# Softmax results of a three-part attention kernel sent to device memory two at a time, and the tiles that hold them

## The chip, the cores and the metric

The kernel runs on one core of a Trainium2 chip. A core has four compute engines, TensorE (PE, matrix products), VectorE (DVE), ScalarE (ACT) and GpSimd (POOL), and SyncE (SP), whose queue issues nearly all transfers here. Sixteen DMA engines carry those out. The time is the device time of one execution in microseconds (us), given as the median of several runs. A profile is taken of one more execution.

## The reference

Sixteen sequences of 128 tokens with 512 features, all in 32-bit floats, go through a decoder layer and then a gated cross attention.

```python
# decoder layer
ln_out = layernorm(hidden_states, ln1_s, ln1_b)
q, k, v = jnp.split(ln_out @ w_qkv + b_qkv, 3, axis=-1)
x = hidden_states + merge_heads(attention(split_heads(q), split_heads(k), split_heads(v), ltor_mask)) @ w_ao + b_ao
ln_out = layernorm(x, ln2_s, ln2_b)
q = ln_out @ w_q + b_q
k, v = jnp.split(encoder_states @ w_kv + b_kv, 2, axis=-1)
x = x + merge_heads(attention(split_heads(q), split_heads(k), split_heads(v), cross_mask)) @ w_co + b_co
x = x + gelu(layernorm(x, ln3_s, ln3_b) @ w1 + b1) @ w2 + b2
# gated cross attention
a = _layer_norm(audio_kv, ln_gamma, ln_beta)
Q, K, V = x @ Wq.T, a @ Wk.T, a @ Wv.T
attn = softmax(where(mask, Q K^T * scale, -inf))
return x + tanh(gate) * ((attn V) @ Wo.T)
```

There are 16 heads of 32 features, and the hidden layer of the MLP has 2,048. `attention` scales the scores, adds a mask, takes a softmax over the keys and multiplies by the values.

## The kernel before

**Stages.** The sequences form four groups of four batches. The decoder's self-attention (sections A0 to A3), its cross attention (B0 to B3), the MLP (C0 to C3) and the gated attention (D0 to D3) follow each other; a section is one group in one attention. A is on the chip from the start to about 300 us, B to about 540, the MLP to about 945, D to the end. Every engine runs its instructions in the order in which the program lists them (class `InOrder`, line 36), so a wait holds up all that stands behind it on the same engine. Many large products are made of seven products of quarters instead of eight, with sums of quarters made beforehand on GpSimd or VectorE (`left_blocks`, `right_blocks`, `token_sums`, lines 346 to 363 and 1004 to 1011).

**Units and steps.** `attend` (line 662) walks through the softmax in steps. A batch has four units, each 128 queries by four heads by 128 keys (128 x 512 numbers, 256 KB); a step begins one unit. For the unit begun in step k:

- at the first step of a batch, TensorE makes the scores of all four units into four banks (`scores`, 523); the next batch's scores need those banks again;
- VectorE scales (and, in D, masks) the scores into a tile of the tag `s` (`scale_unit`, 540). The steps in which a batch's units are scaled stand in `SCALED` (658): unit 0 in the first, 1 and 2 in the second, 3 in the third. In A and B, GpSimd adds the mask in step k;
- in step k+1 ScalarE takes the exponents (`exp_unit`, 560), in k+2 VectorE inverts the sums and GpSimd divides (`norm_unit`, 569), in k+3 VectorE transposes 32 x 32 blocks in place and SyncE writes the tile to device memory (`turn_unit`, 575);
- in step k+5 of an odd unit SyncE reads the pair back with the blocks rearranged (`receive_pair`, 598), which completes the transpose, and TensorE multiplies by the values ten steps after the batch's first (`mix`, 609), into the product `av`.

The last batch of all is transposed by TensorE instead (`turn_by_array`, 585). The block sizes of a write follow from the tile, `[128, 4, 4, 32]`: each of 128 partitions sends four pieces of 128 numbers, 512 bytes.

**Tiles of the tag `s`.** Seven tiles of 2 KB a partition go round in the order of their requests. A request waits until the last reader of the tile's former content is done, for a softmax unit the landing of its write. Besides the units, the MLP's quarters of token sums (`sums_of`, 1067), its quarters of results (`projected_out`, 1172), four transposed hidden states of the last gated group (1412) and the last batch's own tiles take from the same seven.

**Around the MLP's start.** The MLP is a generator whose first pieces are run inside the last cross-attention section (`beside_last_cross`, 1601). In the last step of that section's sixteen, GpSimd makes the first of the token sums (`sx`), in between that step's and the next step's softmax work; the products `h` take them as operands. Its operands are the first group's normalized tokens (`T_C`) and its weights (`w`, and `t` for their sums).

Of the kernel before, what the change touches and what calls it, by code (L numbers as in the profile page):

```python
# [10 lines left out]
F32 = mybir.dt.float32  # L11
# [5 lines left out]
P = 128  # L17
NB = 16
S = 128
Q = 32  # L20
NQ = S // Q
# [3 lines left out]
KC = H // P  # L25
# [28 lines left out]
def decoder_then_gated_cross_attention(ctx: ExitStack, tc: tile.TileContext, a: dict, out: bass.AP):  # L54
    nc = InOrder(tc)
# [3 lines left out]
    work = ctx.enter_context(tc.tile_pool(name="work", bufs=1))  # L59
    dram = ctx.enter_context(tc.tile_pool(name="dram", bufs=1, space=bass.MemoryType.DRAM))  # L60
# [47 lines left out]
    x = [cpool.tile([P, GB, H], F32, tag=f"x{g}", name=f"x{g}") for g in range(NG)]  # L108
# [228 lines left out]
    HF = TG // 2  # L337
# [2 lines left out]

        return [[t[:, 2 * i : 2 * i + 2, j * HF : (j + 1) * HF] for j in range(2)] for i in range(2)]

    def quarter(pool, tag, name, bufs):
        return pool.tile([P, 2, HF], F32, tag=tag, name=name, bufs=bufs)

    def left_blocks(wt, t):


        (a11, a21), (a12, a22) = halves(wt)
        s3, s2, s4, s1 = (*t, a21)[:4]  # L350
        return [a11, a12, s4, a22, s1, s2, s3], [
            (s3, a11, a21, ALU.subtract), (s1, a21, a22, ALU.add), (s2, s1, a11, ALU.subtract),
            (s4, a12, s2, ALU.subtract),
        ]
# [161 lines left out]
    class Batch:  # L516
        def __init__(self, sec, b):
            self.sec, self.b, self.name = sec, b, f"{sec.name}_{b}"

            self.by_array = sec.at_end and b == GB - 1  # L520
            self.sc, self.s, self.mn, self.sum, self.away, self.pT = {}, {}, {}, {}, {}, {}

    def scores(bt):
        sec, t = bt.sec, slice(bt.b * S, (bt.b + 1) * S)
# [12 lines left out]
    def by_head(t):  # L537
        return t.rearrange("p n c j -> p c n j")

    def scale_unit(bt, j):  # L540
        s = work.tile([P, NQ, KC, Q], F32, tag="s", name=f"s_{bt.name}_{j}", bufs=7)
        if bt.by_array:
            s = s.rearrange("p n c j -> p (n c j)").rearrange("p (c n j) -> p n c j", c=KC, n=NQ)
        bt.s[j] = s
        sc = bt.sc.pop(j).rearrange("p (c n k) -> p c n k", c=KC, n=NQ)
        if bt.sec.adds_only:
            bt.mn[j] = least_tile(bt, j)
            bt.sec.mask_and_least(by_head(s), sc, bt.b, bt.mn[j])
        else:
            bt.sec.scale_mask(by_head(s), sc, bt.b)  # L550
# [24 lines left out]
    def turn_unit(bt, j):  # L575
        s = bt.s.pop(j)
        nc.vector.transpose(s, s)

        if j % 2 == 0:
            bt.away[j // 2] = dram.tile([NQ, P, 2, KC * Q], F32, tag="away", name=f"away_{bt.name}_{j}", bufs=4)  # L580
        nc.sync.dma_start(
            out=bt.away[j // 2][:, :, j % 2].rearrange("m p x -> p m x"), in_=s.rearrange("p m c q -> p m (c q)")
        )

    def turn_by_array(bt, j):

        s = by_head(bt.s.pop(j)).rearrange("p c n k -> p c (n k)")
        tp = ps("sc", f"tp_{bt.name}_{j}")
        for c in range(KC):
            nc.tensor.transpose(tp[:, c * S : (c + 1) * S], s[:, c], ident)  # L590
        pT = work.tile([P, KC, NQ, Q], F32, tag="s", name=f"pT_{bt.name}_{j}", bufs=7)
        bt.pT[j] = pT.rearrange("p c n q -> p n c q")
        if j % 2:
            afterwards("act", lambda: nc.scalar.copy(pT.rearrange("p c n q -> p (c n q)"), tp))
        else:
            afterwards("dve", lambda: nc.vector.tensor_copy(pT.rearrange("p c n q -> p (c n q)"), tp))
# [12 lines left out]
    def mix(bt):  # L609
        sec, b = bt.sec, bt.b  # L610
        av = ps("mm", f"av_{bt.name}")
        for c in range(KC):
            for j in range(GB):
                h = c * GB + j
                nc.tensor.matmul(
                    av[j * HD : (j + 1) * HD, c * S : (c + 1) * S], sec.v[:, b, h * HD : (h + 1) * HD],
                    bt.pT[j][:, :, c, :], start=True, stop=True,
                )
        mT = work.tile([P, KC, S], F32, tag="s", name=f"mT_{bt.name}", bufs=7) if bt.by_array else sec.mixed_tile(b)

        def mixed_out():
            if sec.v_bias is None:
                nc.scalar.copy(mT, av.rearrange("p (c q) -> p c q", q=S))
            else:
                for c in range(KC):
                    nc.scalar.activation(
                        mT[:, c], av[:, c * S : (c + 1) * S], AF.Identity, bias=col(sec.v_bias[0], sec.v_bias[1] + c)
                    )

        afterwards("act", mixed_out)  # L630
        bt.mT = mT
# [23 lines left out]
                out.setdefault(step, []).append(job)  # L655
        return out

    SCALED = ((0,), (1, 2), (3,), ())
    NS = GB * GB
    PRODUCTS = [m + GB * b for b in range(GB) for m in (1, 2, 3)]  # L660

    def attend(sections, ready, others, after=None):
# [14 lines left out]
        def step(k, bt=None, jobs=(), ahead=None):  # L677
# [45 lines left out]
            if bt is not None:  # L723
                for j in SCALED[m]:
                    scale_unit(bt, j)
# [332 lines left out]
    def mlp(ml, last_steps):  # L1058

        def turned_tile(g):  # L1060
# [3 lines left out]
                return [t[:, 0:2], t[:, 2:4]]  # L1064
            return [work.tile([P, 2, TG], F32, tag="mask", name=f"T_C{g}_{n}", bufs=2) for n in range(2)]

        def sums_of(g, t):
            s3, s2, s4 = (quarter(work, "s", f"sx{n}_{g}", 7) for n in range(3))
            quarters = [[t[i][:, :, j * HF : (j + 1) * HF] for j in range(2)] for i in range(2)]
            return token_sums(quarters, s3, s2, s4)  # L1070

# [100 lines left out]
        def projected_out(g, p, mm, acc):  # L1172
            mm = mm.rearrange("p (b n) -> p b n", n=HF)
            (x11, x12), (x21, x22) = halves(x[g])
            add, gadd = nc.vector.tensor_tensor, nc.gpsimd.tensor_tensor
            if p == 0:
                acc["m1"] = quarter(work, "s", f"m1_{g}", 7)
                add(acc["m1"], mm, half_row(ml.b2), ALU.add)
                gadd(x11, x11, acc["m1"], ALU.add)
            elif p == 1:  # L1180
                add(x11, mm, x11, ALU.add)
            elif p == 3:
                add(x21, x21, mm, ALU.subtract)
            elif p == 5:
                acc["u2"] = quarter(work, "s", f"u2_{g}", 7)
                add(acc["u2"], mm, acc["m1"], ALU.add)
                gadd(x12, x12, acc["u2"], ALU.add)
            elif p == 6:
                acc["u3"] = quarter(work, "s", f"u3_{g}", 7)
                add(acc["u3"], mm, acc["u2"], ALU.add)  # L1190
                gadd(x21, x21, acc["u3"], ALU.add)
                gadd(x22, x22, acc["u3"], ALU.add)
            elif p == 4:
                m5 = quarter(work, "s", f"m5_{g}", 7)
                add(m5, mm, half_row(ml.db2), ALU.add)
                gadd(x12, x12, m5, ALU.add)
                gadd(x22, x22, m5, ALU.add)
            elif p == 2:
                add(x12, mm, x12, ALU.add)
# [16 lines left out]
        before, acc = None, {}  # L1216
        for n in range(len(steps) + 1):
# [6 lines left out]
            if n < len(steps):  # L1224
                g, i = steps[n]
# [27 lines left out]
            for r in range(7):  # L1253
                if n < len(steps):
                    p = H_ORDER[r]
                    hidden_product(n, p, sides[p], right1[n][p], h)
                if before is not None:
                    p = O_ORDER[r]
# [15 lines left out]
            if n < len(steps):  # L1274
                t = work.tile([P, 3, 2, HF], F32, tag="kT", name=f"sh_{n}", bufs=2)
# [113 lines left out]
    class GatedAttention(Section):  # L1389
# [11 lines left out]

        def hidden_states(self, b, tag="pT"):

            t = work.tile([P, NQ, KC, Q], F32, tag=tag, name=f"x_{self.name}_{b}", bufs=3 if tag == "pT" else 7)
            nc.vector.transpose(by_chunk(t), squares(x[self.g][:, b, :]))
            send(self.x_away, t, b)

        def prepare(self, p):

            g = self.g  # L1410
            if g == 2 and p in (6, 8, 10, 12):
                gates[3].hidden_states(p // 2 - 3, "s")
            if g == 2 and p in (7, 9, 11, 13):
                gates[3].add_void((p - 7) // 2)

            if p in (1, 7):
                self.back, self.part = receiver("xa"[p == 7] + str(g), self.a_away if p == 7 else self.x_away)
            if p in (1, 3, 7, 9):
                for m in range(2):
                    self.part(m + 2 * (p in (3, 9)))  # L1420
            elif p == 4:
                self.xT = act_tile(self.name, "actT" if g == 3 else "enc")
            elif p in (5, 6):
                self.take_hidden(range(2 * (p - 5), 2 * (p - 4)))
# [171 lines left out]
    gates = [GatedAttention(g) for g in range(NG)]  # L1596
# [111 lines left out]
```

## Time and profile before

| | |
|---|---|
| median of three runs | 1166.22 us (1162.94 to 1170.1) |
| the profiled execution | 1168.78 us, span of its instructions 1167.0 |
| granted TensorE clock, mean | 0.994 |
| writes of softmax units | 188 of 256 KB, landing after 3.0 (A), 5.2 (B), 3.7 (D) us in the median |
| reads of pairs | 4 x 94 of 128 KB, 3.0 (A), 3.6 (B), 2.8 (D) us |
| moved by DMA | 259.80 MB, 223 GB/s |

The median landing times are those of the issues whose landing the page could match. The page names instructions by what they write and read: `s_B<-s_B,mask` is a unit of a cross-attention section to which the mask is added, `away_B<-s_B` its write, `pT_B<-away_B` its read. Nearly all instructions bear line 50, the helper that records them, so they are told apart by these names. "PE busy" includes the time in which a matmul runs at a lowered clock; the row PEclk of the slices, or of a window, tells the share of the full clock that was granted. SyncE's instructions only issue; the landing of a transfer is what others wait for.

### The profile page before, as it was taken

What the parts mean: (1) busy time and instruction counts of PE and PEld (TensorE: products, weight loads), DVE (VectorE), ACT (ScalarE), POOL (GpSimd) and SP (SyncE); (2) the same over time, 40 slices, a digit from 0 to 9 for tenths busy, and PEclk for the clock granted to TensorE, in tenths of its full rate; (3) what the DMA queues carried; (4) which work ended last, traced back from release to release, by engine and by line L of the source; (5) the groups of instructions that cost most, each with busy time, mean ns of one, the idle gap of its engine ahead of it and who ended that gap; (6) DMA issues with size and microseconds to landing.
All of it is one profiled execution on the core that took longest, in us unless ns stands there. A gap on an engine that the chain in (4) does not pass through costs nothing. (4 is left out here: it accounts for less than half of the span.)

```text
span 1167.0 us, 22047 instructions
## 1 busy us (share of the span) xinstructions
PE 1134.5 (97%) x7210; PEld 868.3 (74%) x7210; DVE 739.2 (63%) x1894; ACT 605.6 (52%) x2132; POOL 701.5 (60%) x636
## 2 busy tenths in 40 slices
PE   7999999999999999998999999999999999999988
PEld 5877777657575757545788888888888777878866
DVE  7678878797878877876663633543432247767753
ACT  2467667666666766674221333232222247867653
POOL 7698878688868776684333424433341367545973
PEclk9999999999999999999999999999999999999989
DMA  6598979999889879898796696696457728988964
GB/s 227 148 221 220 240 188 222 248 235 267 199 229 208 239 202 255 243 290 252 264 287 235 188 273 197 193 301 224 154 184 249 211 48 229 249 215 251 264 191 163
DMA packets 325266, 259.80 MB, mean 223 GB/s; under 512 B 83544, under 2 KB 280608, under 8 KB 320288
## 3 DMA queue, kind: packets, MB, share of 16 engines
q1 hardware_dynamic: 325112, 258.38, 78.0%
q8 instruction: 58, 0.95, 0.3%
q14 instruction: 56, 0.46, 0.1%
q10 hardware_dynamic: 40, 0.01, 0.0%
HBM read 163.94 MB, written 94.37 MB: 221 GB/s over the span
## 5 line engine op out<-in xcount | busy, mean ns | idle before, releaser
L50 ACT ACTIVATE s_A<-s_A,mn_A 128x128 f32<-128x128 f32 x256 | 99.5, 393 | 51.5 <-issue 37.3
L50 DVE TENSOR_TENSOR h<-h,h 128x512 f32<-128x512 f32 x80 | 54.9, 686 | 112.6 <-PE h L50 112.6
L50 ACT ACTIVATE s_B<-s_B,mn_B 128x128 f32<-128x128 f32 x256 | 99.5, 393 | 46.6 <-issue 32.5
L50 ACT ACTIVATE h<-h 128x512 f32<-128x512 f32 x64 | 40.3, 630 | 160.6 <-DVE h L50 160.6
L50 POOL TENSOR_TENSOR s_D<-s_D,sum_D 128x512 f32<-128x512 f32 x64 | 66.5, 1040 | 67.8 <-DVE sum_D L50 66.3
L50 ACT ACTIVATE s_D<-s_D,mn_D 128x128 f32<-128x128 f32 x256 | 99.2, 392 | 0.4 <-issue 0.4
L50 POOL TENSOR_TENSOR s_B<-s_B,sum_B 128x512 f32<-128x512 f32 x64 | 66.8, 1045 | 48.7 <-DVE sum_B L50 44.3
L50 POOL TENSOR_TENSOR s_A<-s_A,sum_A 128x512 f32<-128x512 f32 x64 | 66.6, 1041 | 36.0 <-DVE sum_A L50 35.3
L50 POOL TENSOR_TENSOR s_A<-s_A,ma 128x512 f32<-128x512 f32 x64 | 81.9, 1280 | 5.4 <-DVE s_A L50 3.7
L50 POOL TENSOR_TENSOR s_B<-s_B,mask 128x512 f32<-128x512 f32 x64 | 81.3, 1270 | 2.1 <-DMA away_B<-s_B 0.4
L50 POOL TENSOR_TENSOR rstd_aD<-rstd_aD,mhalf 128x1 f32<-128x1 f32 x12 | 6.6, 548 | 114.6 <-DVE rstd_aD L50 101.1
L50 POOL TENSOR_TENSOR sh<-h 128x512 f32<-128x512 f32 x32 | 40.7, 1272 | 50.9 <-ACT h L50 43.0
L50 PE MATMUL mo_B<-w_co,mT_B 128*128 128x512 f32 x128 | 60.5, 616 | 2.1 <-ACT mT_B L50 2.1
L50 PE MATMUL h<-T_C,t 128*128 128x256 f32 x256 | 60.7, 380 | 1.4 <-DVE h L50 1.4
L50 PE MATMUL h<-T_C,w 128*128 128x256 f32 x256 | 61.0, 381 | 0.8 <-DVE h L50 0.8
L50 PE MATMUL h<-sx,t 128*128 128x256 f32 x256 | 60.6, 380 | 0.0
L50 PE MATMUL o<-w,h 128*128 128x256 f32 x256 | 60.5, 379 | 0.0
L50 PE MATMUL o<-t,h 128*128 128x256 f32 x256 | 60.5, 379 | 0.0
L50 PE MATMUL o<-t,sh 128*128 128x256 f32 x256 | 60.5, 379 | 0.0
L50 PE MATMUL mo_A<-w_ao,mT_A 128*128 128x512 f32 x128 | 59.1, 604 | 0.0
L50 DVE CUSTOM_DVE_ANT_0 s_D<-sc_D,gmask 128x128 f32<-128x128 f32 x256 | 57.2, 283 | 0.9 <-DMA turned_x<-x_D 0.9
L50 PE MATMUL mm_q_B<-T_B,w_cq 128*128 128x512 f32 x128 | 57.3, 595 | 0.0
(324 smaller groups left out, 2986.1 us busy)
## 6 DMA issues: line engine op xcount, KB each, us to landing
t<-kept SPq DMA_DIRECT2D x24, 1024.0 KB, 6.9
away_A<-s_A SPq DMA_DIRECT2D x64, 256.0 KB, 3.0
pT_A<-away_A SPq DMA_DIRECT2D x128, 128.0 KB, 3.0
away_B<-s_B SPq DMA_DIRECT2D x64, 256.0 KB, 5.2
pT_B<-away_B SPq DMA_DIRECT2D x128, 128.0 KB, 3.6
away_D<-s_D SPq DMA_DIRECT2D x60, 256.0 KB, 3.7
pT_D<-away_D SPq DMA_DIRECT2D x120, 128.0 KB, 2.8
w<-in_L_xattn_w_dram SPq DMA_DIRECT2D x24, 512.0 KB, 5.6
```

The lines of the kernel that those rows point to most:

```text
L50: return lambda *args, **kw: self.tc.keep_in_program_order(call(*args, **kw))
```

## The change

A tile of the tag `s` now holds two units, and there are three such tiles (12 KB a partition). The seventh 2 KB have a tag of their own, `xh`, with one tile, taken in turn by one of the MLP's quarters, by the four transposed hidden states, and by the last batch's mixed values. The two units of a pair lie beside each other within each of four blocks, so that one write of 512 KB, issued after the odd unit's transpose, takes both in pieces of 1,024 bytes; the even unit's write, a step earlier, is gone. `SCALED` moves unit 2 of a batch from its second to its third step. In the MLP the quarters no longer go round: groups 0 and 2 have three fixed places and groups 1 and 3 three others, and the result quarters m1, u2, u3 and m5 of a group take the places of its token sums.

```diff
     def scale_unit(bt, j):
-        s = work.tile([P, NQ, KC, Q], F32, tag="s", name=f"s_{bt.name}_{j}", bufs=7)
-        if bt.by_array:
-            s = s.rearrange("p n c j -> p (n c j)").rearrange("p (c n j) -> p n c j", c=KC, n=NQ)
+        if j % 2 == 0:
+            shape = [P, 2, KC, NQ, Q] if bt.by_array else [P, NQ, 2, KC, Q]
+            bt.pair = work.tile(shape, F32, tag="s", name=f"s_{bt.name}_{j}", bufs=3)
+        s = bt.pair[:, j % 2].rearrange("p c n j -> p n c j") if bt.by_array else bt.pair[:, :, j % 2]
+        bt.pair_of[j] = bt.pair
         bt.s[j] = s
...
         nc.vector.transpose(s, s)
-        if j % 2 == 0:
-            bt.away[j // 2] = dram.tile([NQ, P, 2, KC * Q], F32, tag="away", name=f"away_{bt.name}_{j}", bufs=4)
-        nc.sync.dma_start(
-            out=bt.away[j // 2][:, :, j % 2].rearrange("m p x -> p m x"), in_=s.rearrange("p m c q -> p m (c q)")
-        )
+        pair = bt.pair_of.pop(j)
+        if j % 2:
+            away = dram.tile([NQ, P, 2, KC * Q], F32, tag="away", name=f"away_{bt.name}_{j}", bufs=4)
+            nc.sync.dma_start(
+                out=away.rearrange("m p u x -> p m (u x)"), in_=pair.rearrange("p m u c q -> p m (u c q)")
+            )
+            bt.away[j // 2] = away
...
-    SCALED = ((0,), (1, 2), (3,), ())
+    SCALED = ((0,), (1,), (2, 3), ())
...
+        places = []
+
+        def place(g, n):
+            return places[3 * (g % 2) + n]
+
         def sums_of(g, t):
-            s3, s2, s4 = (quarter(work, "s", f"sx{n}_{g}", 7) for n in range(3))
+            if g < 2:
+                for n in range(1 + g):
+                    t2 = work.tile([P, 2, 2, HF], F32, tag="s", name=f"sx_{g}_{n}", bufs=3)
+                    places.extend((t2[:, 0], t2[:, 1]))
+                if g == 0:
+                    places.append(work.tile([P, 2, HF], F32, tag="xh", name="sx_0", bufs=1))
+            s3, s2, s4 = place(g, 0), place(g, 1), place(g, 2)
...
-                acc["m1"] = quarter(work, "s", f"m1_{g}", 7)
+                acc["m1"] = place(g, 0)
...
-                acc["u2"] = quarter(work, "s", f"u2_{g}", 7)
+                acc["u2"] = place(g, 1)
...
-                acc["u3"] = quarter(work, "s", f"u3_{g}", 7)
+                acc["u3"] = place(g, 2)
...
-                m5 = quarter(work, "s", f"m5_{g}", 7)
+                m5 = place(g, 0)
...
-            t = work.tile([P, NQ, KC, Q], F32, tag=tag, name=f"x_{self.name}_{b}", bufs=3 if tag == "pT" else 7)
+            t = work.tile([P, NQ, KC, Q], F32, tag=tag, name=f"x_{self.name}_{b}", bufs=3 if tag == "pT" else 1)
...
-                gates[3].hidden_states(p // 2 - 3, "s")
+                gates[3].hidden_states(p // 2 - 3, "xh")
```

The last batch's transposed pairs (`pT` in `turn_by_array`) take two-unit tiles of the tag `s` in the same manner, and its `mT` takes `xh`.

More of the change, by code (lines that the diff above doesn't have):

```diff
@@ L341, in halves @@
         return [[t[:, 2 * i : 2 * i + 2, j * HF : (j + 1) * HF] for j in range(2)] for i in range(2)]
-    def quarter(pool, tag, name, bufs):
-        return pool.tile([P, 2, HF], F32, tag=tag, name=name, bufs=bufs)
     def left_blocks(wt, t):
@@ L520, in __init__ @@
             self.by_array = sec.at_end and b == GB - 1
-            self.sc, self.s, self.mn, self.sum, self.away, self.pT = {}, {}, {}, {}, {}, {}
+            self.sc, self.s, self.mn, self.sum, self.away, self.pT, self.pair_of = {}, {}, {}, {}, {}, {}, {}
     def scores(bt):
@@ L590, in turn_by_array @@
             nc.tensor.transpose(tp[:, c * S : (c + 1) * S], s[:, c], ident)
-        pT = work.tile([P, KC, NQ, Q], F32, tag="s", name=f"pT_{bt.name}_{j}", bufs=7)
+        if j % 2 == 0:
+            bt.pair = work.tile([P, 2, KC, NQ, Q], F32, tag="s", name=f"pT_{bt.name}_{j}", bufs=3)
+        pT = bt.pair[:, j % 2]
         bt.pT[j] = pT.rearrange("p c n q -> p n c q")
@@ L618, in mix @@
                 )
-        mT = work.tile([P, KC, S], F32, tag="s", name=f"mT_{bt.name}", bufs=7) if bt.by_array else sec.mixed_tile(b)
+        mT = work.tile([P, KC, S], F32, tag="xh", name=f"mT_{bt.name}", bufs=1) if bt.by_array else sec.mixed_tile(b)
         def mixed_out():
```

## The prediction

> **What bounds the kernel now.** I read the busy sums first, then the slices, then TensorE's waits, and at last the order in time around the places where TensorE stops.
>
> ```profile
> PE 1134.5 (97%) x7210; PEld 868.3 (74%) x7210; DVE 739.2 (63%) x1894; ACT 605.6 (52%) x2132; POOL 701.5 (60%) x636
> DMA  6598979999889879898796696696457728988964
> ```
>
> TensorE works 1134.5 of 1167.0 us; 32.5 us are its gaps. Some 7 us of them are the start (4.4 us for the first load, the rest for the first transposes) and are not touched, so some 25 us could be won by any change, plus what a slow clock costs after a gap. The second line shows where the 16 DMA engines are nearly full: windows of 20 us give a DMA share of 0.97 to 1.03 at 220 to 280 and 480 to 520 us, and of 0.97 to 0.98 at 1000 to 1040. From 580 to 940 us (the MLP) TensorE is busy 360.00 of 360 us: nothing can be won there.
>
> TensorE's own waits (engine, what it waited for, us, times, longest):
>
> ```profile
> PE sc_D L50 <- DVE mn_D L50: 4.3, 3, 3.2
> PE av_D L50 <- DMA pT_D<-away_D: 3.3, 2, 2.7
> PE av_B L50 <- DMA pT_B<-away_B: 2.4, 2, 1.6
> PE mo_B L50 <- ACT mT_B L50: 2.1, 1, 2.1
> ```
>
> Only 5.7 us are waits for the softmax results' way through device memory, the thing that the change makes cheaper. The first line is VectorE's scaling of scores, which the change delays for one unit in four.
>
> **1. The transfers, part by part.** Before, 188 writes of 256 KB in pieces of 512 bytes; after, 94 of 512 KB in pieces of 1,024. By the trace's packets a piece of 512 bytes takes 27 ns (median), one of 1,024 bytes 46 ns. 188 x 512 pieces x 27 ns / 16 engines = 162 us; 94 x 512 x 46 / 16 = 138 us: 24 us less of 16 engines' time, 0.26 us a pair. Steps last 3.8 us in the decoder and 3.1 us in the gated part (the scalings' spacing), a pair two of them, so the load falls by 3 to 4%. SyncE issues 94 instructions less, 0.38 us each, but most stood in time in which SyncE waited for a landing anyway.
>
> [...]
>
> What a pair's landing does: the odd unit's write now carries both, so where the queue was empty it lands 46 x 32 - 27 x 32 = 0.6 us later; where the queue was full the even unit's 0.86 us no longer stand ahead and it lands 0.26 us sooner. The reads are unchanged. The reads of a pair land 4 to 8 us ahead of their matmuls in most batches of the decoder, so 0.6 us is covered there. In the gated part five batches have under 0.7 us to spare or none; bounds -0.3 to +0.6 each, -1.5 to +3 us; I take +0.5.
>
> **2. Three tiles of two instead of seven of one.** Before, a unit's tile was free again three or four steps after its write; now the pair scaled from step 2i needs the write issued at step 2i-2 to have landed. I matched VectorE's scalings and transposes and SyncE's writes by their order. In the 90 pairs with a predecessor, the landing that a pair would need comes after its scaling 13 times, by 9.2 us in all (decoder 3.7, gated 5.4); with 0.6 us more for each landing the sum is 18.4. But they come in groups (82 to 96, 265 to 281, 490 to 525, 987 to 1030 us) where SyncE itself lags 2 to 5 us behind the transposes, and within a group one wait serves for all: the largest are 0.8, 1.5, 0.6 and 2.0, 5 to 7 us of VectorE's waiting. Behind a waiting scaling stand the next step's evictions and transposes. VectorE is busy 63% and comes to its evictions before TensorE does, so a wait under 1.8 us (a product of eight quarter matmuls, its rows 1.72 us apart) passes unseen. Bounds 0 and 18.4; I take +1, nearer the group maxima less that cover.
>
> **3. Unit 2 scaled a step later.** Four instructions of 0.21 us each move behind a wait: at 1128.72 TensorE's scores wait 3.16 us for unit 3's scaling, which now stands behind unit 2's 0.85 us; before, those ran while VectorE idled 2.02 us for a GpSimd result. The same at 971.81 (0.90). +0.85 twice: +1.5, bounds 0 and 1.7. In the decoder a batch has a whole further step to free its banks: 0.
>
> **4. The MLP's first token sums.** Before, the first of GpSimd's sums took the tile of unit 121 of 128, landed at 525.7. Now it takes the pair of units 122 and 123, whose second write was issued at 528.58 and landed at 533.16. GpSimd and TensorE there:
>
> ```profile
> 528.14 1.27 POOL L50 TENSOR_TENSOR sx<-T_C 128x512 f32<-128x512 f32 x1
> 529.50 1.27 POOL L50 TENSOR_TENSOR T_C<-T_C 128x512 f32<-128x512 f32 x1
> 530.72 1.04 POOL L50 TENSOR_TENSOR s_B<-s_B,sum_B 128x512 f32<-128x512 f32 x1
> 531.72 1.26 POOL L50 TENSOR_TENSOR s_B<-s_B,mask 128x512 f32<-128x512 f32 x1
> 532.95 1.26 POOL L50 TENSOR_TENSOR sx<-T_C 128x512 f32<-128x512 f32 x1
> ```
>
> ```profile
> 527.55 5.19 PE L50 MATMUL mo_B<-w_co,mT_B 128*128 128x512 f32 x8 [2.12 <-ACT mT_B L50]
> 532.58 1.89 PE L50 MATMUL h<-T_C,w 128*128 128x256 f32 x8
> 534.31 1.95 PE L50 MATMUL h<-sx,t 128*128 128x256 f32 x8
> 536.21 0.41 PE L50 MATMUL av_B<-pT_B,v_B 128*32 128x128 f32 x4
> 538.23 1.07 PE L50 MATMUL av_B<-pT_B,v_B 128*32 128x128 f32 x28 [1.60 <-DMA pT_B<-away_B]
> ```
>
> The second sum was ready at 534.21, a tenth before its product began at 534.31. If the first starts at 533.2 instead of 528.14, what is queued behind it on GpSimd (the in-place sum, a softmax division, a mask, the second sum, 6.07 us from the first's start) ends at 539.3: TensorE waits 4.9 us. The matmuls behind it waited 1.6 us for a read before, which is now covered, so 3.2 us remain at that place. After the gap of 2.12 us the same eight matmuls of 512 took 5.19 us instead of 3.70, and the clock row of 528 to 532 us reads 0.68: a gap there costs 1.5 us more. The three later stops for VectorE (0.42, 0.79, 0.98) can take up to 2.2 of this back. Bounds +0 (the write lands 5 us sooner) and +6.6 (3.2 and the 3.4 us of clock lost at 1128 to 1136, rows 0.50 and 0.66); I take +4.
>
> [...]
>
> **5. The rest at nothing, with its cover.** The strided division, transposes and exponents keep their counts; the transposes of the hidden states already work on 32-element pieces and take 0.70 us like the contiguous ones, so 0; for the division the mask's 1.27 against 1.04 us is the upper end, 188 x 0.23 = 43 us of a GpSimd busy 60%, which TensorE would hardly see. Four hidden-state transposes share one tile: the fourth, at 984.91, waits for a landing at 986.99; the scaling behind it waited for that same landing before (0.88), so VectorE loses 1.2 us, TensorE 0 to 1.2; I take 0. The MLP's later quarters rest on waits that TensorE does not see (360.00 of 360). The last batch's transposed pairs take tiles long free.
>
> **Sum:** +0.5 +1 +1.5 +4 = +7, less some 1 us for fuller queues that drain sooner around 520 and 1010 (a fifth of the 5.7 us of waits for reads): +6. The profiled execution took 1168.78 us (span 1167.0, 1.78 around it), so it would become 1174.8; it stood 2.56 above the median of three runs, 1166.22, which becomes **1172**.
>
> **Rivals.** *The queues win.* In the crowded stretches the lighter writes pull every landing forward; the waits for reads (5.7), the 2.12 behind them and 1.7 us of clock at each of 524 to 532 and 1026 to 1034 go, and the new wait at 528 with them: up to 11 us, about half of it likely, 1160. For it: shares of 1.0 there. Against it: a landing takes 3 to 5 us and only 0.26 of it falls. It decides if the write of units 122 and 123 lands before 528. Chance 0.17. *Too few tiles.* The waits of part 2 do not hide: SyncE's reads wait for a landing, its next write stands behind them, VectorE behind that, and all 18.4 us reach TensorE with part 4: about 1186. For it: SyncE waits 34.7 us in 28 cases for the gated writes' landing. Against: the 4 to 8 us ahead of the matmuls. Chance 0.2. *Nothing moves*, because the MLP's start takes its delay back: 1166, chance 0.18. The forecast, 1168 to 1178, has 0.45.
>
> The range, 1161 to 1186, reaches to the middle of the first rival and of the second. A measurement of this kernel tells about 1% (11.7 us) from no change. Faster by that (under 1154.6) needs all of the first rival and more: 0.04. Slower (over 1177.9): the second rival and an edge of the forecast, 0.21. Within: 0.75.
>
> **What would show it.** Right: 94 writes; VectorE's scalings waiting for landings in the four groups, 5 to 7 us in all; the first sum starting after 531; a gap of 3 to 5 us before the product of the second sum and a clock row under 0.8 behind it; the gap before the last scores near 4.0. Wrong: the first sum near 528, shorter waits for reads, or scalings that wait in nearly every pair of the gated part.

## The result, and the profile after

The changed kernel takes 1182.12 us in the median of six runs (1180.21 to 1188.25), the kernel before 1165.61 in six (1162.94 to 1170.6): a ratio of **1.0148**, with a 95% interval of 1.0129 to 1.0168. The prediction said 1172, some 6 us more; it became 17 us more. The side and the range were right, the size was a third of what came.

The profiled execution of the changed kernel took 1182.27 us, with a span of 1180.5 against 1167.0. The busy sums, the DMA slices and the group of the gated scalings, from the page after:

```profile
PE 1140.7 (97%) x7210; PEld 871.4 (74%) x7210; DVE 740.0 (63%) x1894; ACT 607.2 (51%) x2132; POOL 703.2 (60%) x636
DMA  6597868888888779997696696695457618787864
L50 DVE CUSTOM_DVE_ANT_0 s_D<-sc_D,gmask 128x128 f32<-128x128 f32 x256 | 57.2, 284 | 24.7 <-DMA away_D<-s_D 24.6
```

TensorE ran the same 7,210 matmuls in 6.2 us more busy time (1134.5 before); of the 13.5 us of span the other 7.3 are gaps. Some 3.5 us of the busy time are a lowered clock: the mean granted clock is 0.991 as against 0.994, which by the clock's records is 10.3 us lost as against 6.8. The fourth to fourteenth DMA slices (88 to 409 us) read 89799998898 before and 78688888887 now, and the time of all packets adds up to 25 us less of 16 engines' time (24 were forecast): the pieces of 1,024 bytes do cost the engines less. The third line is the large change. Before, VectorE's gated scalings waited 0.9 us in all, and not for a write of results; now 24.6 us, all for the landing of one. The same group before:

```profile
L50 DVE CUSTOM_DVE_ANT_0 s_D<-sc_D,gmask 128x128 f32<-128x128 f32 x256 | 57.2, 283 | 0.9 <-DMA turned_x<-x_D 0.9
```

TensorE's waits after (engine, what it waited for, us, times, longest):

```profile
PE h L50 <- POOL sx L50: 5.5, 1, 5.5
...
PE av_D L50 <- DMA pT_D<-away_D: 4.3, 5, 1.7
PE sc_D L50 <- DVE mn_D L50: 4.0, 3, 3.2
...
PE mo_B L50 <- ACT mT_B L50: 2.7, 1, 2.7
PE av_B L50 <- DMA pT_B<-away_B: 1.3, 1, 1.3
```

The one large newcomer is the product of the MLP's token sum. The waits for reads, which the lighter writes might have shortened, add up to 5.6 us, as against 5.7.

**Where the time came from.** I matched TensorE's products of the two profiles one by one and read how far each product after lies behind its counterpart before. By the end of the decoder (scores at 515 us) TensorE is 1.6 us late, across the MLP's start it loses 7.5 more, in the MLP nothing, in the gated part 4.2: 13.3 of the 13.5 us.

The MLP's start, first SyncE's issues of the changed kernel (start, duration, engine, operation, names, count):

```profile
523.38 0.38 SPq L50 DMA_DIRECT2D away_B<-s_B  x1
523.80 1.77 SPq L50 DMA_DIRECT2D w<-in_L_xattn_w_dram  x2
528.96 1.75 SPq L50 DMA_DIRECT2D pT_B<-away_B  x4
530.81 0.38 SPq L50 DMA_DIRECT2D kept_v_D<-v_D  x1
531.23 0.43 SPq L50 DMA_DIRECT2D w<-in_L_xattn_w_dram  x1
531.76 0.42 SPq L50 DMA_DIRECT2D away_B<-s_B  x1
```

This is a loop. The joint write of units 120 and 121 is issued at 523.38 and lands at 528.89 (by its semaphore). The four reads of that pair stand next on SyncE and start at 528.96. The joint write of units 122 and 123, transposed since 526.80, stands behind them and goes out at 531.76; it lands at 537.46. Before, the write of unit 121 alone landed at 525.70, so the reads began at 525.77, the next odd write at 528.58, and it landed at 533.16. SyncE's issues of before:

```profile
521.00 0.38 SPq L50 DMA_DIRECT2D away_B<-s_B  x1
...
525.77 1.75 SPq L50 DMA_DIRECT2D pT_B<-away_B  x4
...
528.58 0.41 SPq L50 DMA_DIRECT2D away_B<-s_B  x1
```

Each round passes its delay to the next: 3.2 us at the first landing, 4.3 at the second.

GpSimd and TensorE of the changed kernel at the same place:

```profile
537.52 1.26 POOL L50 TENSOR_TENSOR sx<-T_C 128x512 f32<-128x512 f32 x1 [6.58 <-DMA away_B<-s_B]
538.87 1.26 POOL L50 TENSOR_TENSOR T_C<-T_C 128x512 f32<-128x512 f32 x1
540.08 1.04 POOL L50 TENSOR_TENSOR s_B<-s_B,sum_B 128x512 f32<-128x512 f32 x1
541.08 1.26 POOL L50 TENSOR_TENSOR s_B<-s_B,mask 128x512 f32<-128x512 f32 x1
542.30 1.27 POOL L50 TENSOR_TENSOR sx<-T_C 128x512 f32<-128x512 f32 x1
```

```profile
530.21 6.16 PE L50 MATMUL mo_B<-w_co,mT_B 128*128 128x512 f32 x8 [2.66 <-ACT mT_B L50]
536.20 1.89 PE L50 MATMUL h<-T_C,w 128*128 128x256 f32 x8
543.62 3.78 PE L50 MATMUL h<-sx,t 128*128 128x256 f32 x8 [5.53 <-POOL sx L50]
547.33 1.79 PE L50 MATMUL av_B<-pT_B,v_B 128*32 128x128 f32 x32
```

The first sum starts 0.06 us after the landing, the second is done at 543.57, and TensorE starts the product at 543.62. The gap is 5.53 us, and the eight matmuls behind it take 3.78 us instead of 1.95: of the 4 us from 544 the granted clock is 0.50. TensorE falls back 2.0 us ahead of the gap (the `mo_B` matmuls took 6.16 instead of 5.19), 7.5 by the gap and the slow product, and recovers 2.0 behind them, where the kernel before had its own waits: the 7.5.

SyncE's waits grew in all three sections. Its waits for landings of writes, of the changed kernel and below them of the kernel before:

```profile
SPq L50 <- DMA away_D<-s_D: 73.8, 29, 4.4
SPq L50 <- DMA away_B<-s_B: 61.9, 28, 4.7
SPq L50 <- DMA away_A<-s_A: 58.1, 31, 5.0
```

```profile
SPq L50 <- DMA away_D<-s_D: 34.7, 28, 2.9
SPq L50 <- DMA away_B<-s_B: 33.0, 20, 7.1
SPq L50 <- DMA away_A<-s_A: 23.3, 18, 3.3
```

The mean times of the odd unit's write, from the end of the odd unit's transpose to the issue, and from the issue to the landing (us, matched by order, the landing by its semaphore):

| | A | B | D |
|---|---|---|---|
| before, to the issue | 1.12 | 1.28 | 1.41 |
| after, to the issue | 1.09 | 1.33 | 2.88 |
| before, issue to landing | 3.48 | 4.01 | 3.46 |
| after, issue to landing | 3.99 | 4.45 | 3.97 |

From its issue the joint write takes about half a microsecond longer to land in every section. In the crowded stretches that the prediction names it is no better: 4.67 instead of 3.81 us at 220 to 280, 5.23 instead of 4.18 at 480 to 520, 4.13 instead of 3.64 at 1000 to 1040 (the same 5 to 7 pairs each). Its issue is later on the mean in D alone; in A and B SyncE waits longer without its writes going out later.

### The profile page after: what moved, and what is told of

It reads as the page before. It is cut to its first block, busy times and chain, and to the rows that moved or that the text cites. A ratio compares the mean times of both kernels' runs of the same rounds, so it can differ in the third digit from the quotient of the medians.

```text
span 1180.5 us, 21820 instructions
## 1 busy us (share of the span) xinstructions
PE 1140.7 (97%) x7210; PEld 871.4 (74%) x7210; DVE 740.0 (63%) x1894; ACT 607.2 (51%) x2132; POOL 703.2 (60%) x636
## 4 chain that ended last, share of the span: by engine, by line
PE 48%; POOL 4%; DMA 3%; issue 2%; DVE 1%; ACT 1%; SPq 1%; POOLq 0%; DVEq 0%; ACTq 0%
PE h L50 16%; PE o L50 16%; PE mm_q_D L50 4%; PE mm_v_D L50 2%; PE mm_k_D L50 2%; PE mo_B L50 2%; DMA away_D<-s_D 1%; POOL s_D L50 1%; PE mo_D L50 1%; PE mm_o_D L50 1%; PE sc_D L50 1%; PE av_D L50 1%; POOL sums_mT L50 1%; POOL x L50 1%; PE mm_v_B L50 1%
## 5 line engine op out<-in xcount | busy, mean ns | idle before, releaser
L50 DVE CUSTOM_DVE_ANT_0 s_D<-sc_D,gmask 128x128 f32<-128x128 f32 x256 | 57.2, 284 | 24.7 <-DMA away_D<-s_D 24.6
L50 POOL TENSOR_TENSOR x<-x,sx 128x512 f32<-128x512 f32 x24 | 30.5, 1284 | 66.1 <-DVE sx L50 66.1
L50 PEld LDWEIGHTS h<-sx,t 128*128 128x128 f32 x256 | 49.5, 194 | 13.5 <-POOL sx L50 5.9
```

Of the source, the lines that this page charges most:

```text
L50: return lambda *args, **kw: self.tc.keep_in_program_order(call(*args, **kw))
```

## The experiments

The questions: is it the joint write, the three tiles, the place of the token sums or the order of scaling? Theory A said that the place of the first token sum is what costs at the MLP's start, its rival B that the softmax work or the late landing holds TensorE there whatever the order; theory C that the joint writing lengthens SyncE's chain and makes the landings late, its rival D that fewer or paired tiles are the cost, whoever writes them; rival E that it is the order of scaling.

Columns of the summary: TensorE's delay against the kernel before, in the one profiled execution of each, split at the end of the decoder, at the MLP's start and over the gated part; the ratio is from all runs. The profiled execution of before was some 3 us slower than its median, so the sum of a row mostly lies below what its ratio says; that of kernel 5 was 4 us faster than its own median, that of kernel 7 5 us slower. A column is good to some 2 us: kernels 1 and 11 have the gated part of the changed kernel, instruction for instruction, and theirs read +6.3 and +5.6 against its +4.2. A difference of two ratios is good to some 3 us. There is no kernel 8.

| kernel | decoder | MLP's start | gated | ratio, 95% interval |
|---|---|---|---|---|
| after | +1.6 | +7.5 | +4.2 | 1.0148 (1.0129 to 1.0168) |
| 1: first sum in the free tile | +3.6 | +2.7 | +6.3 | 1.0117 (1.0094 to 1.0139) |
| 2: pair tiles, each unit written alone | +1.2 | +2.2 | +2.4 | 1.0079 (1.0058 to 1.0099) |
| 3: before, with the new order of scaling | -0.5 | -0.2 | -0.2 | 1.0015 (0.9999 to 1.0030) |
| 4: six unit tiles, fixed quarters, new order | +0.2 | -0.3 | -1.6 | 1.0016 (0.9997 to 1.0035) |
| 5: 4, reads behind the write | +3.3 | -1.2 | +2.9 | 1.0115 (1.0096 to 1.0134) |
| 6: 2, first sum in the free tile | +1.7 | -0.6 | -0.4 | 1.0023 (1.0009 to 1.0036) |
| 7: after, reads behind the write | +12.7 | +1.9 | +4.8 | 1.0166 (1.0144 to 1.0188) |
| 9: after, joint time but pieces of 512 B | +3.5 | +7.3 | +10.1 | 1.0208 (1.0190 to 1.0227) |
| 10: after, reads behind in the gated part only | +1.5 | +6.5 | +2.5 | 1.0111 (1.0088 to 1.0133) |
| 11: after, last 16 decoder units written alone | +2.1 | +3.3 | +5.6 | 1.0106 (1.0083 to 1.0128) |
| 12: 1, 10 and 11 together | +3.4 | 0.0 | +1.8 | 1.0051 (1.0030 to 1.0072) |
| 13: 6, old order of scaling | +0.6 | -0.2 | +4.4 | 1.0061 (1.0039 to 1.0082) |

**The order of scaling alone (3).** The kernel before with one line of the change:

```diff
-    SCALED = ((0,), (1, 2), (3,), ())
+    SCALED = ((0,), (1,), (2, 3), ())
```

> The kernel before with one edit: unit 2 of each batch scaled in the batch's third step instead of its second. The prediction's part 3 puts this at +1.5 us: ratio 1.000 to 1.002, the gap before the last batch's scores 4.0 instead of 3.16 us, TensorE's total wait for VectorE's minima 4.3 to 6 us. Rival E (the order of the scalings is behind the unforeseen part, by the decoder's mask additions and exponents that now wait for unit 2): ratio above 1.004.

Measured: 1.0015. The gap before the last scores, in its TensorE timeline:

```profile
1127.46 2.89 PE L50 MATMUL sc_D<-k_D,q_D 32*128 32x128 f32 x28 [3.82 <-DVE mn_D L50]
```

Before it was 3.16 with 0.21 a moment earlier: the gap grew by some 0.5 us. By the interval the edit costs 0 to 3.5 us by itself, so a cost of none is not excluded.

**Unit tiles (4).** The changed kernel with its new order, fixed quarters and the tile `xh`, but six tiles of one unit, each unit written when it is turned:

```diff
-        if j % 2 == 0:
-            bt.pair = work.tile(shape, F32, tag="s", name=f"s_{bt.name}_{j}", bufs=3)
+        s = work.tile([P, NQ, KC, Q], F32, tag="s", name=f"s_{bt.name}_{j}", bufs=6)
```

> The changed kernel, its scaling order, its fixed quarters and the tile `xh`, but six tiles of one unit in place of three of two, and each unit written by itself in pieces of 512 bytes. Theory C and the prediction's part 2 together: a unit's tile is free one step earlier than a pair's and no write is joint, so the waits for landings mostly go: ratio 1.001 to 1.005, the rest being the scaling order and the token sums, whose second place is still the tile of unit 123. Rival D (fewer tiles cost, in pairs or not): ratio 1.010 or more, with VectorE's waits for landings in the gated part near 20 us.

Measured: 1.0016, no loss at the MLP's start, and 0.4 us of VectorE's waits for landings in the gated part. Six units' room in place of seven, the fixed places and the shared tile cost nothing that can be seen beyond what the order of scaling costs (1.0015; both intervals are some 2 us wide to either side).

**Pair tiles, written singly (2), and the first sum's place (1, 6).** Kernel 2 is the changed kernel with

```diff
-        if j % 2:
-            away = dram.tile(...)
-            nc.sync.dma_start(out=away..., in_=pair...)
+        if j % 2 == 0:
+            bt.away[j // 2] = dram.tile(...)
+        nc.sync.dma_start(out=bt.away[j // 2][:, :, j % 2]..., in_=s...)
```

> The changed kernel with its three tiles of two units, but each unit written by itself after its transpose, 256 KB in pieces of 512 bytes as before. Theory C (the joint write lengthens the chain on SyncE's queue: landing of a write, reads of that pair, next write, because all 512 KB now land after the odd unit's transpose): landings of the odd units' writes fall by about 1 us in the crowded stretches, the write of units 122 and 123 lands 2 to 5 us earlier against TensorE's work, and VectorE's waits for landings in the gated part fall from 24.6 us to under 12; 4 to 8 us faster than the changed kernel, ratio to before 1.008 to 1.011. Rival D (three tiles of two are the cost, whoever writes them): the waits stay, ratio 1.013 to 1.017.

Kernel 1 is the changed kernel with the first sum of the first group in `xh` and the other two in a pair tile:

```diff
             if g < 2:
+                if g == 0:
+                    places.append(work.tile([P, 2, HF], F32, tag="xh", name="sx_0", bufs=1))
                 for n in range(1 + g):
...
-                if g == 0:
-                    places.append(work.tile([P, 2, HF], F32, tag="xh", name="sx_0", bufs=1))
```

> The changed kernel with one edit: the first of group 0's token sums takes the free tile `xh`, and the second and third the pair's two halves. The changed kernel's profile has the first sum wait 6.58 us for the write of units 122 and 123 (landing 537.46 us) and TensorE wait 5.53 us for the second. Theory A (the place of the first sum is what costs at the MLP's start): the first sum, the in-place sum, a division and a mask run before the landing, only the second sum waits for it; TensorE's wait falls from 5.5 to about 1 us, with 1.5 us of lost clock less: 5 to 7 us faster than the changed kernel, ratio to the kernel before 1.009 to 1.011. Rival B (the softmax tail behind the sums, or the late landing itself, holds TensorE at the MLP's start whatever the order): less than 2 us faster, ratio 1.013 to 1.016.

Kernel 6 has both edits:

> Three tiles of two units, each unit written alone in pieces of 512 B (1.0079 of the time before, +9.2 us), and the first of the MLP's sums in the free tile of the hidden states. What is left of the change is that two units come free together. Theory G (a pair of units comes free with its later write): the MLP's start loses 0 to 0.7 us instead of 2.2 us, the last gated stage still loses about 2.4 us, ratio 1.0055 to 1.0070. Rival: the sum's place has no part in it once the writes are single, ratio 1.0075 to 1.0085.

Measured: 1.0079 for the writes alone, a little below theory C's range, 1.0117 for the place alone, between theory A and its rival, and 1.0023 for both, lower than either side had expected. So the joint write costs 0.7% (after less 2) to 0.9% (1 less 6), 8 to 11 us, and the first sum's place 0.3% to 0.6%, 4 to 7 us. In kernel 2 the first sum starts at 532.76, where the single write of unit 123 lands (532.70), while the profile puts that wait down to a load of `w` that the sum does not read: the releaser named there was a guess by time. In kernel 6 GpSimd makes the first sum without a wait, as before the change, and the second, which now takes a place of the pair, just behind the landing of unit 123's write (534.74):

```profile
529.56 1.27 POOL L50 TENSOR_TENSOR sx<-T_C 128x512 f32<-128x512 f32 x1
...
534.86 1.27 POOL L50 TENSOR_TENSOR sx<-T_C 128x512 f32<-128x512 f32 x1 [0.46 <-POOL s_B L50]
```

```profile
528.97 3.70 PE L50 MATMUL mo_B<-w_co,mT_B 128*128 128x512 f32 x8 [1.81 <-ACT mT_B L50]
532.51 1.89 PE L50 MATMUL h<-T_C,w 128*128 128x256 f32 x8
536.18 1.99 PE L50 MATMUL h<-sx,t 128*128 128x256 f32 x8 [1.78 <-POOL sx L50]
```

The gap is 1.78 us (none before) and the matmuls behind it run at 1.99; `mo_B` took 3.70 instead of 5.19, so the place as a whole loses nothing. With this order of scaling, two units in one tile are nearly free, if each is written as soon as it is turned.

**Joint in time, but small pieces (9).** The changed kernel with its one write cut in two by unit, both issued after the odd unit:

```diff
-            nc.sync.dma_start(out=away.rearrange("m p u x -> p m (u x)"), in_=pair.rearrange(...))
+            for u in range(2):
+                nc.sync.dma_start(out=away[:, :, u]..., in_=pair[:, :, u]...)
```

> The changed kernel, both units of a pair still written after the second is turned, but by two transfers of 256 KB in pieces of 512 B instead of one of 512 KB in pieces of 1,024 B. It keeps the joint time of writing and drops the larger pieces. Theory J (what costs is that the first unit's bytes wait for the second unit): landings as late as the changed kernel's or later by up to 0.5 us, ratio 1.013 to 1.019. Rival P (one transfer of 512 KB in large pieces is itself what lands late): the landings come back to those of the kernel before and the ratio falls to 1.006 to 1.010.

Measured: 1.0208, above what either theory gave, and well on the side of theory J. VectorE's waits in it:

```profile
DVE s_D L50 <- DMA away_D<-s_D: 26.8, 20, 3.3
...
DVE s_B L50 <- DMA away_B<-s_B: 9.2, 5, 2.5
```

Kernel 9 differs from kernel 2 (1.0079) in when the first unit is written: it is the first unit's waiting for the second that costs, and the one larger write is the better of the two joint ways: 0.6% or 7 us. Whether the size of the pieces or the one issue less (0.38 us of SyncE in the loop) does it, this pair of kernels does not tell apart. From the end of the odd unit's transpose to the landing kernel 9 needs 6.01, 6.57 and 7.25 us in A, B and D, the changed one 5.07, 5.78 and 6.84; all of that lies ahead of the issue (0.7 to 1.2 us more), and from issue to landing kernel 9 is 0.2 to 0.4 us quicker. That speaks for SyncE's queue, but does not show it. For the pieces' size speak the 27 and 46 ns of a piece of 512 and of 1,024 bytes and the 25 us of engine time that the larger pieces saved.

**Reads behind the write (5, 7, 10).** If SyncE's loop is the mechanism, it opens when the write of a step goes out ahead of the reads. Kernels 5 (on 4) and 7 (on the changed one):

```diff
-            if pair % 2 and 0 <= pair < by_transfer(len(units)):
-                receive_pair(*units[pair])
...
                 (turn_unit if k - 3 < by_transfer(k) else turn_by_array)(*units[k - 3])
+            if pair % 2 and 0 <= pair < by_transfer(len(units)):
+                receive_pair(*units[pair])
```

> The kernel of six unit tiles and fixed quarters again (each unit written alone, 1.0016 of the time before), with one move: SyncE issues the two reads of a pair after the step's write instead of ahead of it. Theory L (SyncE's order is a loop: a write that lands late holds the reads, the reads hold the next write): the time from the turned tile to the issue of its write in the last gated stage falls from 2.00 us to under 0.5 us, nothing else grows, and the ratio is 0.996 to 1.001. Rival R (the reads are what is short): the reads go out later, TensorE's waits for the read-back tiles grow by more than is gained, ratio 1.003 or more.

> The changed kernel with one move: SyncE issues the reads of a pair after the joint write of the step instead of ahead of it. Theory L (the joint write is late because it stands behind reads that wait for the last joint write): the time from the turned tile to the issue of the joint write in the last gated stage falls from 2.88 us to under 0.6 us, VectorE's waits for landings there from 24.6 us to under 8 us, the landing for the MLP's first sum comes up to 1 us sooner, and the ratio falls from 1.0148 to 1.004 to 1.010. Rival R (the tiles are short, whatever SyncE's order): the waits for landings stay over 15 us and the ratio is 1.012 or more.

Measured: 1.0115 and 1.0166. The write's own delay went as theory L said: in the gated part from 2.00 to 0.14 us (5) and from 2.88 to 0.10 us (7), and VectorE's waits for landings in kernel 7 left the list. But the time got worse, for the reason that rival R of kernel 5 gave (rival R of kernel 7, that the tiles are short, expected VectorE's waits to stay, and they went): from the landing of the write to the landing of the last read it now takes 8.6 to 10.5 us instead of 4.6 to 6.1, and TensorE waits for the reads. TensorE's waits of kernel 7:

```profile
PE av_D L50 <- DMA pT_D<-away_D: 6.3, 5, 4.3
PE av_B L50 <- DMA pT_B<-away_B: 4.9, 4, 1.6
```

Of the 19.5 us of kernel 7 in its profiled execution, 11 are lost between 250 and 515 us and 6 at one place, the first gated batches (978 to 984 us); after that it gains 1.1 on the kernel before. So kernel 10 moves the reads only there:

```diff
+            late = ready and k >= 12
-            if pair % 2 and 0 <= pair < by_transfer(len(units)):
+            if not late and pair % 2 and 0 <= pair < by_transfer(len(units)):
                 receive_pair(*units[pair])
...
+            if late and pair % 2 and 0 <= pair < by_transfer(len(units)):
+                receive_pair(*units[pair])
```

> The changed kernel; in the last gated stage alone, from its step 12 on, SyncE issues the reads of a pair after the joint write of the step instead of ahead of it. It leaves the decoder and the start of the gated stage as they are, which is where the move cost TensorE its reads. Theory L (in the gated stage the joint write stands behind reads that wait for the last joint write, and the late landing holds the pair tiles): VectorE's waits for landings of away_D there fall from 24.6 us to under 8 us, the gated stage's net loss of 4.2 us against the kernel before falls to 0 to 2 us, and the ratio from 1.0148 to 1.011 to 1.013. Rival T (three tiles of two are too few, whenever the write is issued): the waits stay over 15 us and the ratio within 1.014 to 1.016.

Measured: 1.0111 (its interval just meets that of the changed kernel). SyncE's waits in it for landings of gated writes, and below them two of all engines' waits:

```profile
SPq L50 <- DMA away_D<-s_D: 6.9, 3, 3.0
```

```profile
POOL s_D L50 <- DMA pT_D<-away_D: 6.7, 3, 2.4
...
DVE s_D L50 <- DMA away_D<-s_D: 0.5, 1, 0.5
```

VectorE's 24.6 us are down to 0.5 with the same three tiles: the tiles were not too few as such, the writes went out too late. TensorE got back 1.7 of 4.2 us in the profile and some 4 us by the ratios. It now waits 5.5 us for reads in place of 4.3, which may be why it did not get back all; both figures are near their own scatter.

**The MLP's start alone (11), and all three together (12).** Kernel 11 writes only the last section of the decoder unit by unit:

```diff
+        if bt.single:
+            ...  # both halves of the pair as in kernel 2
+        elif j % 2:
...
+                bt.single = last and not ready
```

> The changed kernel; only the last 16 units of the decoder are written one by one, in pieces of 512 B, each as soon as it is turned. The pair tiles, the sums' places and the joint writes everywhere else stay. Theory M (the loss at the MLP's start is the late landing of the last joint writes): the wait of TensorE for the first token sum falls from 5.5 us to some 3.5 us, the net loss at the MLP's start from 7.5 us to 2 to 3 us, and the ratio from 1.0148 to 1.009 to 1.012. Rival Q (the joint writes of all the decoder before it have set TensorE and the queues back by then): the start of the MLP still loses 5 us or more, ratio 1.013 or more.

> The changed kernel with three of its costs taken away together: the first token sum in the free tile of the hidden states, the last 16 units of the decoder written one by one, and the gated stage's reads behind its joint writes from step 12 on. Joint writes in pieces of 1,024 B stay in three quarters of the decoder and in the gated stage. If the account by these three places is complete, what is left is 0 to 5 us, ratio 1.000 to 1.005, and the larger pieces themselves bring nothing that can be seen. If it is not, ratio 1.007 or more, with a loss that grows along the decoder. If the larger pieces gain where nothing waits for them, under 0.999.

Measured for 11: 1.0106, with the start of the MLP at +3.3 us. Its TensorE timeline:

```profile
530.69 6.64 PE L50 MATMUL mo_B<-w_co,mT_B 128*128 128x512 f32 x8 [3.22 <-ACT mT_B L50]
537.17 1.89 PE L50 MATMUL h<-T_C,w 128*128 128x256 f32 x8
541.51 2.00 PE L50 MATMUL h<-sx,t 128*128 128x256 f32 x8 [2.45 <-POOL sx L50]
```

The write of unit 123 lands at 535.34, and the first sum starts at 535.41. The gap for the sum is down to 2.45 and its matmuls take 2.00 us, at a granted clock of 1.00. So the 16 last units' joint writing carries more than half of the loss at the MLP's start. What is left is near kernel 2's 2.2, in which no write is joint: what the joint writes of the decoder before add there is 1 us, within the scatter of the column.

Kernel 12 came to 1.0051: the start of the MLP costs nothing, the gated part 1.8 us. Of its other 3.4 us, 2.0 are there at the first scores of all (40 us), before a result is written. The account by three places is nearly complete (1.0051, where at most 1.005 was expected); a gain from the larger pieces where nothing waits for them is not to be seen in any column.

**The old order of scaling on pair tiles (13).** Kernel 6 with the line of kernel 3 reversed.

> Three tiles of two units, each unit written alone, the first token sum in the free tile (1.0023 of the time before), and unit 2 scaled a step earlier, as in the kernel before. If the three edits add up, the new order of scaling (1.0015 alone) is most of what was left: ratio 0.999 to 1.002. If the earlier scaling fills the pair tiles sooner and so brings VectorE's waits for landings back, ratio 1.003 or more.

Measured: 1.0061, worse than kernel 6 by 0.4%. VectorE's waits for landings, in all engines' waits of kernel 13:

```profile
DVE s_D L50 <- DMA away_D<-s_D: 9.2, 6, 2.8
DVE s_A L50 <- DMA away_A<-s_A: 8.1, 7, 2.8
```

In kernel 6 they are 4.0 and 3.5 us. Unit 2 opens the second pair of a batch; asked for a step earlier, its tile is more often not yet free. The later scaling, which in kernel 3 gained nothing, is what the pair tiles need. No kernel of these beats the one before.

## Why the prediction was wrong in size

The runs put sizes beside the terms of the sum. From the kernel before to kernel 6 (pair tiles, new order, fixed quarters) it is 2.7 us, where parts 2 and 3 gave +1 and +1.5; from 6 to 2 (the first sum's place) 6.5 us, where part 4 gave +4; from 2 to the changed kernel (the joint writing) 8 us, where part 1 gave +0.5, less 1 for fuller queues. Taken the other way round, the joint writing is 11 us and the place 4. The joint writing is the step that failed.

**Part 1, the transfers, failed, and it carried the rest.** Of the full queue the prediction said that "the even unit's 0.86 us no longer stand ahead and it lands 0.26 us sooner", and it took off some 1 us for "fuller queues that drain sooner". The joint write landed 0.51, 0.44 and 0.51 us later after its issue in A, B and D, and 0.5 to 1.0 us later in the three crowded stretches. The saving of engine time was right (25 us, 24 forecast); I had taken it for a saving in the time to land. The +0.6 us that I had worked out for an empty queue was near the mark on the mean of all writes. And I had costed the landing only at its reads ("4 to 8 us ahead of their matmuls"), although a rival named the loop: reads wait for the landing, the next write stands behind the reads. SyncE's waits doubled (34.7 to 73.8 us in D), the joint write of D went out 1.5 us later, and that is what parts 2 and 4 then met.

**Part 2, three tiles of two, was too small by its input.** From landings as they were I had 5 to 7 us of VectorE's waiting and +1 for TensorE. With the landings as they became, it was 24.6 us in D alone, beyond the 18.4 that I had as the bound for all sections, in 20 of its 30 pairs, close to the sign that I had named as showing me wrong. It reached TensorE only in part: at most 4.2 us in D and 1.6 in the decoder. Kernels 2 and 6 show the tiles' part (VectorE's gated waits 4.5 and 4.0 us), kernel 10 that an earlier issue takes the waits away.

**Part 3, unit 2 a step later, was wrong within the change.** Alone it is 1.7 us (kernel 3: 1.0015) against +1.5, but the interval holds no cost as well, the one gap that was to grow by 0.85 us grew by 0.5, and in the profile the gated part lost nothing: that the sizes agree is luck as much as insight. And I added it as if the terms were independent. Kernel 13 shows that on pair tiles the later scaling saves 4 us, so the 2.7 us of kernel 6 agree with +1 and +1.5 by luck too: pair tiles in the old order cost 7 us. Part 5's "nothing" for fixed quarters and the shared tile holds in kernel 4.

**Part 4, the token sums, had the right place and mechanism and the wrong size.** Predicted: the first sum at 533.2, a gap of 4.9 us, +4. Measured: 537.52, 5.53 us, +7.5. The landing that I used was that of the kernel before; the write went out 3.2 us later by the loop and took 1.1 us longer. But TensorE itself came 3.6 us later to its product, so the gap is only 0.6 us longer than forecast. The slow clock behind it cost 1.8 us, near the 1.5 that I had, and the give-back was 2.0, inside my 1.6 (the read) to 3.8 (with the three later stops). What the term lacked most is the 2.0 us that TensorE lost ahead of the gap, half of them a lower clock at `mo_B`. My upper bound, 6.6, had a clock loss in it but not these.

**The rivals.** "Too few tiles", 1186, came nearer (1182.12) than the forecast. Its chain (SyncE's reads wait, the next write behind them, VectorE behind that) was real, as kernels 7 and 10 show. Its arithmetic was not, and that the number came near is luck: over half of the loss in the profile was at the MLP's start, and TensorE passed most of VectorE's 24.6 us unseen. "The queues win" found nothing: the write that decides it landed at 537.46, not before 528.

## What to carry to other kernels

Here, merging two transfers made the first one's bytes wait for the second one's work (the joint time alone, kernel 9 against kernel 2: 1.0208 against 1.0079). A read and then the next write stood in order behind that landing on one queue, so the delay went round (in D 2.88 us to the issue, 1.41 before), and the 25 us less of engine time did not buy it back. When a change delays an event, redo the later steps with the new time of the event before costing them: landings read from the old trace are inputs that the change itself moves. Edits that share a buffer are not terms of a sum: an order that gains nothing alone may be what the new buffers need, and the first consumer of a shared tile after a phase ends is the place to look at first.

## What the runs showed that I had not expected

**The clock after a gap did not follow the gap alone.** The same eight matmuls `mo_B` at the MLP's start took 3.70 us after gaps of 1.81 (6), 1.86 (3) and 2.26 us (12), but 5.19 after 2.12 (before), 5.40 after 1.20 (5), 6.16 after 2.66 (after), 6.64 after 3.22 (11) and 5.16 after 4.10 us (13). So the loss is there behind a gap of 1.20 us and absent behind one of 2.26. In the profiles of before and after the granted clock falls to 0.50 for 3.4 or 6.8 us at a time (3.4, 3.4 and 6.8 before, three times 6.8 after), and the matmuls lose by the part of such a stretch that they meet: after, it lasts from 528.36 to 535.18 us, `mo_B` runs in 4.97 us of it and takes 2.46 us longer than 3.70. In all but one of thirteen profiles (those of the table but for kernel 7, and that of before) a second gap, before the last 28 matmuls of `av_B`, stands a few microseconds ahead (1.52 us in kernel 5; none in kernel 2). The two gaps together sort the thirteen: some 2.4 to 2.66 us where `mo_B` took 3.70 us, 2.72 us and more where it took 5.16 or longer. That margin is small and no run varied it alone, so it is a pattern to test, not a rule shown.

**A larger write landed later even where the queue had been full**, by 0.5 to 1.0 us in the three crowded stretches (DMA shares of 0.96, 1.00 and 0.98 before, 0.91, 0.98 and 0.84 after), although its pieces cost the engines a seventh less time (46 ns in place of twice 27).

**VectorE waited 25 us without TensorE losing more than a few**: 24.6 us of its waits in D came with 4.2 us of TensorE's delay, and taking away nearly all of them (kernel 10, with later reads) gave back 1.7 in the profile and some 4 by the ratios.
